# Convolutions and a wavelet layer on one core: a third buffer for stored results, kept sums in more tiles and asked for sooner, 12 ScalarE products in the first mixing

## The chip, the cores and the metric

The kernel runs on one core of one Trainium2 chip. The metric is the device time of one execution in microseconds (us); lower is better. TensorE (PE) multiplies matrices into PSUM, VectorE (DVE) and ScalarE (ACT) do elementwise work, GpSimd (POOL) does a little of it, and SyncE (SP) issues most of the DMAs; ACT issues the rest.

## The reference

The input is `x` of shape (4, 64, 256, 256): 4 batches of 64 channels of 256x256 images. Four layers follow each other. Layers 0, 1 and 3 are long convolutions whose kernel is separable (an outer product of two filters that a small network makes); layer 2 is a thresholding in the Haar wavelet domain that mixes channels. Cut to what matters:

```python
# layers 0, 1 and 3, for each channel
k = hx[:, None] * hy[None, :]                 # separable 256x256 kernel
y = irfft2(rfft2(x, 512x512) * rfft2(k, 512x512) / 512)[:256, :256]
x = y + x * bias[:, None, None]

# layer 2
f1 = haar2d(x)
acc = 0
for i in range(2):
    f4 = einsum('bchw,oc->bohw', f1 * v[i], conv_w[i])
    acc += sign(f4) * relu(abs(f4) - tau[i])
x = haar2d(acc, inverse=True) + x
```

## The kernel before, in words

Each convolution is written as two products with Toeplitz matrices, one for each axis. `contract` (L250) does one product of a 256x256 channel as four matmuls into one PSUM bank; `toeplitz` (L241) loads the filter's matrix, 256 KB, with a DMA on SP. `first` (L256) is the product of the first axis (`pa`) and ScalarE's copy of it to SBUF (`a`, L267). `second` (L271) is the product of the second axis (`py`) and the residual sum on VectorE (`y`, L284), which writes a tile of the tag that it is given, with `BUFS[tag]` buffers.

The work has three kinds of stages.

- `convolutions(b, ...)` does layers 0 and 1 of batch b, channel by channel, and the forward Haar transform. `pairs` (L327) splits the result into sums and differences of neighbours; `store` (L332) keeps both in DRAM (`keep`) for the inverse. `levels` goes on with the row transform, `split` and `rest` divide the values into two parts for TensorE, `down` transforms the columns, and `away` (L382) copies the coefficients from PSUM into a tile of tag "co" (L385) and stores them from SP (L386).
- `mixing(b, ...)` does the mixing of channels and the threshold in 64 groups of positions. It loads `f` (tag "f", 3 buffers, L423), multiplies by the channel matrix into PSUM (`px`, L441), and scales the 16 products of a group: `scaled` (L458) on VectorE takes the first 16 - n_act of them in one instruction (L460), `scaled_too` (L462) on ScalarE takes the other n_act with one activation of 128x64 each (L465). The results are in `f4` (tag "f4", 2 buffers). `size`, `sign`, `shrink`, `signed` and `add` finish the threshold. n_act comes from `N_ACT`, one number for each batch.
- `inverse(b, ...)` transforms back and does layer 3. For each channel, `sooner` asks for the filter, `early` (L513) loads the kept sums `r` (L515), `fetch` copies the coefficients on ScalarE (`zc`, L525), `rows` transforms them on TensorE (`pw`, L532 and L533), and `join` (L552) on VectorE adds the kept sums and makes the image `u` (L554, L557, L558). For the first 16 channels `halves` (L536, tag "f4") and `cols` come in between. Then layer 3 follows: product, copy, product, sum (L284, into tag "co" again), and the store of the output from ACT's queue (L602). In batches 0 to 2 every third channel is put off: its `u` goes to DRAM from ACT's queue (L562), and layer 3 for it is done beside the last mixing (`convolution`, L605).

The stages of different batches overlap. While batch b is mixed, the convolutions of batch b+1 are worked off beside it, and their last coefficients are formed during the inverse of batch b.

The order of the work is written out as events. Each step is entered with `at(time, run, unit)`; the time is the tick of its channel or group plus an offset from the table `PLACE` (L26). The events are sorted by time and run, and that gives each instruction its rank. A planner in the framework then simulates the engines with its own costs and lets an instruction pass others of its queue where these are not ready or their buffer is not free yet. So a `PLACE` is a rank and not a promise, and a change of buffers can move other instructions too. On the chip each engine and each DMA queue works in the planned order and waits by semaphores. Tiles of one tag take turns in its buffers; a new tile waits until the last use of the old one has ended.

For `early`, `PLACE` is counted from the channel's tick c after the inverse begins. `join` stands at c + 1.433, and one tick later for the first 16 channels. The same tag "f" with its 3 buffers serves the mixing's loads and the kept sums of the inverse.

Of the kernel before, what the change touches and what calls it, by code (L numbers as in the profile page):

```python
# [9 lines left out]
F32 = mybir.dt.float32  # L10
# [7 lines left out]
P = 128  # L18
ROW = S + P

GT = 4
BUFS = {"res": 1, "y": 5, "co": 2}

N_ACT = (14, 12, 12, 6)

PLACE = {  # L26
    "load": 0.714,
# [22 lines left out]
    "shrink": 1.777,  # L50
    "signed": 2.802,
    "add": 3.331,
    "sooner": -0.8,
    "early": -0.4,
    "fetch": 0.414,
    "rows": 1.071,
    "halves": 1.522,
# [41 lines left out]
def conv_seq_kernel(ctx, tc, x, fz, fw, bias, decay, haar, haar_row, factors, vt, taut, wmix, out):  # L99
# [14 lines left out]
    nc = tc.nc  # L114
# [8 lines left out]
    mx = ctx.enter_context(tc.tile_pool(name="mx", bufs=2))  # L123
# [117 lines left out]
    def toeplitz(layer, c, name):  # L241

        t = tp.tile([P, 2, S], F32, name=name, tag="toep")
        nc.sync.dma_start(t, ap(pads[layer], c * 2 * ROW, [[1, P], [ROW, 2], [1, S]]))
        return t
# [25 lines left out]
    def second(b, st, key, layer, res, new, tag, ahead=None):  # L271
# [9 lines left out]
        def residual(c):  # L281
            s = st[c]
            y = io.tile([P, 2, S], F32, name=f"{new}_{b}_{c}", tag=tag, bufs=BUFS[tag])
            nc.vector.scalar_tensor_tensor(y, s[res], bsb[:, layer, c : c + 1], s["p" + new], ALU.mult, ALU.add)  # L284
# [9 lines left out]
    def level(n, chunk, begin=0, count=None):  # L294

        count = n if count is None else count
        v = z.rearrange("p n s x c -> p n s (x c)")[:, chunk].rearrange("p (j e s) x -> p j e s x", e=2, s=P // 2 // n)
        halve(v[:, begin : begin + count, 0, 0, :], v[:, begin : begin + count, 1, 0, :])

    def butterfly():  # L300

        v = z.rearrange("p n s (h k) c -> p n s h k c", k=2)
        for h in range(2):
            halve(v[:, :, 0, h, 0, :], v[:, :, 0, h, 1, :])
# [6 lines left out]
    def at(time, run, unit):  # L311
        events.append((time, len(events), run, unit))

    def convolutions(b, ticks, in_parts=(), border=None):
# [67 lines left out]
        def away(c):  # L382
            t = io.tile([P, 2, S], F32, name=f"co_{b}_{c}", tag="co", bufs=BUFS["co"])
            ps = parts.pop(("ps", c)).rearrange("p e (k w) -> p e k w", k=2)
            nc.scalar.copy(t.rearrange("p k (e w) -> p e k w", e=2), ps)  # L385
            nc.sync.dma_start(coef[b][:, c].rearrange("k p w -> p k w"), t)  # L386
# [122 lines left out]
    def inverse(b, start, put_off):  # L509

        st = {}

        def early(c):  # L513
            r = mx.tile([P, 2, 2, P], F32, name=f"r_{b}_{c}", tag="f", bufs=3)
            nc.sync.dma_start(r, keep[b][c])  # L515
            st[c]["r"] = r

        def sooner(c):
            st[c] = {}
            if c not in put_off:  # L520
                st[c][2] = toeplitz(2, c, f"t2_{b}_{c}")

        def fetch(c):
            a = mx.tile([P, 2, 2, P], F32, name=f"zc_{b}_{c}", tag="mag")
            nc.scalar.copy(a.rearrange("p h k i -> p (h k) i"), z[:, c // 16, :, :, c % 16].rearrange("p i x -> p x i"))  # L525
            st[c]["z"] = a

        def rows(c):
            a = st[c]["z"]
            ps = psx.tile([P, 2, 2, 2, P], F32, name=f"pw_{b}_{c}", tag="mix")[:, 0]  # L530
            for m in range(2):
                nc.tensor.matmul(ps[:, 0, m, :], a[:, 0, m, :], hsinv, start=True, stop=True)  # L532
                nc.tensor.transpose(ps[:, 1, m, :], a[:, 1, m, :], ident)  # L533
            st[c]["pw"] = ps

        def halves(c):  # L536
            w = st[c]["w"] = mx.tile([P, 2, 2, 2, P], F32R, name=f"w_{b}_{c}", tag="f4")
            ps = st[c]["pw"]
            nc.scalar.copy(w[:, 0], ps)  # L539
            nc.vector.tensor_tensor(w[:, 1], ps, w[:, 0].bitcast(F32), ALU.subtract)  # L540

        def cols(c):
            ps = psm.tile([P, 2, 2, P], F32, name=f"pu_{b}_{c}", tag="mm")
            flat = "p e m w -> p (e m w)"
            for i in range(2):
                nc.tensor.matmul(
                    ps.rearrange(flat), hb, st[c]["w"][:, i].rearrange(flat), start=(i == 0), stop=(i == 1)
                )
            st[c]["pw"] = ps

        def join(c):
            ps = st[c]["pw"]  # L552
            t = io.tile([P, 2, 2, P], F32, name=f"t_{b}_{c}", tag="res", bufs=BUFS["res"])
            nc.vector.scalar_tensor_tensor(t, st[c]["r"], 0.5, ps, ALU.mult, ALU.add)  # L554
            u = io.tile([P, 2, S], F32, name=f"u_{b}_{c}", tag="y", bufs=BUFS["y"])
            v = u.rearrange("p m (w e) -> p m w e", e=2)
            nc.vector.tensor_add(v[:, :, :, 0], t[:, 0], t[:, 1])  # L557
            nc.vector.tensor_sub(v[:, :, :, 1], t[:, 0], t[:, 1])  # L558
            st[c]["u"] = u

        def aside(c):
            nc.scalar.dma_start(late[b, c], st.pop(c)["u"])  # L562

        along = start - groups - 3

        def when(tick, n, chunk, *span):
            at(tick + PLACE["level"], lambda _: level(n, chunk, *span), 0)

        at(along + 11 + PLACE["level"], lambda _: butterfly(), 0)
        for chunk in range(1, 4):  # L570
            turn = start + 16 * (chunk - 1)
            for n in (1, 2, 4, 8):
                when(along + 12 + 3 * chunk if b + 1 < B else turn, n, chunk)
            when(turn + 1, 16, chunk)
            for i in range(2):
                when(turn + 2 + 2 * i, 32, chunk, 16 * i, 16)
            for i in range(4):
                when(turn + 6 + 2 * i, 64, chunk, 16 * i, 16)

        for c in range(C):  # L580
            for name, stage in zip(("sooner", "early", "fetch", "rows"), (sooner, early, fetch, rows)):
                at(start + c + PLACE[name], stage, c)
            turn = start + c
            if c < 16:
                at(start + c + PLACE["halves"], halves, c)
                at(start + c + PLACE["cols"], cols, c)
                turn += 1
            at(turn + PLACE["join"], join, c)
            if c in put_off:
                at(turn + PLACE["aside"], aside, c)  # L590
            else:
                shift = (0.0, 0.0)
                if put_off:
                    shift = ((-0.27, -0.342), (0.23, 0.158))[c % 3]
                for name, stage in zip(("a3", "a3 copy", "y3", "y3 sum", "out"), last(b, st)):
                    at(turn + PLACE[name] + shift[name[0] != "a"], stage, c)

    def last(b, st):
        return [
            *first(b, st, "u", 2, "a3"),  # L600
            *second(b, st, "a3", 2, "u", "y3", "co"),
            lambda c: nc.scalar.dma_start(out[b, c].rearrange("(k p) w -> p k w", p=P), st.pop(c)["y3"]),  # L602
        ]
# [42 lines left out]
    for b in range(B):  # L646
        mixing(b, start, N_ACT[b])
        end = start + groups + 3
# [124 lines left out]
```

## Time and profile before

| what | value |
|---|---|
| time, median of 3 runs | 2897.4 us (2896.96 to 2901.36) |
| profiled execution, own time | 2897.57 us |
| its span, first to last instruction | 2895.8 us |
| instructions in it | 52461 |
| PE busy | 2825.5 us |
| DVE busy | 2501.4 us |
| ACT busy | 2082.3 us |
| POOL busy | 335.3 us |
| HBM traffic over the span | 223 GB/s |
| granted TensorE clock | 0.999 of full speed |

The span is that of one profiled execution, and the time around it is the launch and the end. Busy time of an engine is the time in which at least one of its instructions runs; "idle before" is the time that the engine stood before an instruction, and a releaser is what ended that wait by the semaphores. SPq and ACTq are the DMA issues of these two queues. The stages follow each other in the trace: mixing 0 from 446 to 865 us, inverse 0 to 1067, mixing 1 to 1518, inverse 1 to 1726, mixing 2 to 2177, inverse 2 to 2378, mixing 3 to 2666, and inverse 3 to the end.

### The profile page before, as it was taken

The page shows a single profiled execution, that of the slowest core. Times are in us where ns is not written, and L with a number is a line of the kernel's source. Part 1 is how long each engine was busy: PE and PEld are TensorE (multiplying, and loading weights), DVE is VectorE, ACT ScalarE, POOL GpSimd, SP SyncE. Part 2 cuts the span into 40 slices and gives each one's busy share as a digit, 9 for nine tenths or more (in the row PEclk, how much of TensorE's full clock was granted, in tenths as well). Part 3 has the DMA queues.
Part 4 walks back from the last instruction along what each step waited for, and adds up shares of the span by engine and source line. Part 5 has one row for each costly group of instructions (what it writes and reads, how often), then busy time and mean ns, then how long its engine had stood idle before and what let it go on. Part 6 is the DMA issues. An engine that isn't in the chain of part 4 may idle for free. (4 is left out here: it accounts for less than half of the span.)

```text
span 2895.8 us, 52461 instructions
## 1 busy us (share of the span) xinstructions
PE 2825.5 (98%) x16566; PEld 2548.3 (88%) x16566; DVE 2501.4 (86%) x4263; ACT 2082.3 (72%) x4950; POOL 335.3 (12%) x644
## 2 busy tenths in 40 slices
PE   8999999999999999999999899999999999999999
PEld 6999998888888898998888898998888898888998
DVE  4656558999999779999998679999999779999985
ACT  2333338999995558989985558989995558888554
POOL 0111111121121001221211001121121000000000
PEclk9999999999999999999999999999999999999999
DMA  5877777666677886777777886777767888777776
GB/s 163 261 231 231 231 232 223 207 202 207 194 209 225 271 260 199 215 211 212 208 214 234 258 265 196 214 212 211 212 207 235 269 276 239 230 237 208 217 239 207
DMA packets 599368, 649.78 MB, mean 224 GB/s; under 512 B 48465, under 2 KB 517044, under 8 KB 598964
## 3 DMA queue, kind: packets, MB, share of 16 engines
q1 hardware_dynamic: 519860, 562.09, 65.9%
q10 hardware_dynamic: 79232, 84.34, 8.3%
q8 instruction: 134, 2.20, 0.3%
q14 instruction: 142, 1.16, 0.1%
HBM read 426.77 MB, written 219.48 MB: 223 GB/s over the span
## 5 line engine op out<-in xcount | busy, mean ns | idle before, releaser
L253 PE MATMUL py<-t,a 128*128 128x256 f32 x3072 | 924.1, 383 | 18.6 <-ACT a L267 18.0
L267 ACT COPY a<-pa 128x512 f32<-128x512 f32 x768 | 492.0, 641 | 510.8 <-PE pa L254 450.4
L465 ACT ACTIVATE f<-px,vt 128x64 f32<-128x64 f32 x2816 | 623.1, 410 | 95.0 <-DVE f L460 94.7
L254 PEld LDWEIGHTS py<-t,a 128*128 128x128 f32 x3072 | 584.0, 190 | 79.6
L254 PE MATMUL py<-t,a 128*128 128x128 f32 x3072 | 590.5, 274 | 0.0
L253 PEld LDWEIGHTS py<-t,a 128*128 128x128 f32 x3072 | 495.9, 191 | 62.9 <-ACT a L267 31.7
L441 PE MATMUL px<-wb,f 128*128 128x256 f32 x2048 | 490.4, 381 | 11.9 <-ACT f L465 11.7
L441 PEld LDWEIGHTS px<-wb,f 128*128 128x128 f32 x2048 | 367.8, 190 | 57.2 <-ACT f L465 18.4
L343 POOL TENSOR_TENSOR sd<-less 128x128 f32<-128x128 f32 (+4 forms) x320 | 187.4, 586 | 1874.9 <-DVE less L342 1535.2
L525 ACT COPY zc<-z 128x512 f32<-128x512 f32 x256 | 281.4, 1103 | 106.9 <-PE pw L533 93.4
L476 DVE TENSOR_TENSOR mag<-mag,vt 128x1024 f32<-128x1024 f32 x256 | 317.0, 1238 | 10.2 <-ACT mag L469 9.4
L469 ACT ACTIVATE mag<-f 128x1024 f32<-128x1024 f32 x256 | 304.7, 1190 | 22.1 <-DVE z L486 21.6
L480 DVE SCALAR_TENSOR_TENSOR mag<-mag,f 128x1024 f32<-128x1024 f32 x256 | 317.1, 1240 | 0.1
L253 PE MATMUL pa<-t,y 128*128 128x256 f32 x1024 | 308.3, 383 | 5.8 <-DVE y L284 5.0
L253 PE MATMUL pa<-t,x 128*128 128x256 f32 x1024 | 305.8, 380 | 0.0
L366 DVE TENSOR_TENSOR sp<-sd,sp 128x512 fp32r<-128x512 f32 x256 | 179.9, 703 | 132.3 <-ACT sp L361 130.6
L472 ACT ACTIVATE f<-f 128x1024 f32<-128x1024 f32 x256 | 291.8, 1140 | 3.1
L253 PE MATMUL pa<-t,u 128*128 128x256 f32 x772 | 231.9, 382 | 4.4 <-ACT w L539 2.9
L284 DVE SCALAR_TENSOR_TENSOR y<-x,bsb,py 128x512 f32<-128x512 f32 x256 | 190.5, 744 | 41.2 <-PE py L254 40.2
L254 PEld LDWEIGHTS pa<-t,y 128*128 128x128 f32 x1024 | 194.5, 190 | 26.3
L254 PEld LDWEIGHTS pa<-t,x 128*128 128x128 f32 x1024 | 194.6, 190 | 26.3
L284 DVE SCALAR_TENSOR_TENSOR y<-y,bsb,py 128x512 f32<-128x512 f32 x256 | 190.4, 744 | 27.8 <-PE py L254 27.8
(72 smaller groups left out, 4426.3 us busy)
## 6 DMA issues: line engine op xcount, KB each, us to landing
t<-pad SPq DMA_DIRECT2D x768, 256.0 KB, 4.0
x<-in_x SPq DMA_DIRECT2D x256, 256.0 KB, 3.8
coef<-co SPq DMA_DIRECT2D x256, 256.0 KB, 3.2
f<-coef SPq DMA_DIRECT2D x256, 256.0 KB, 3.1
r<-keep SPq DMA_DIRECT2D x256, 256.0 KB, 3.9
out_y<-y ACTq DMA_DIRECT2D x256, 256.0 KB, 4.0
keep<-sums SPq DMA_DIRECT2D x256, 128.0 KB, 2.8
keep<-sd SPq DMA_DIRECT2D x256, 128.0 KB, 2.8
```

The source lines that it names most:

```text
L253: nc.tensor.matmul(ps[:, m, :], src[:, 0, m * P : (m + 1) * P], t[:, ::-1], start=True, stop=False)
L254: nc.tensor.matmul(ps[:, m, P:], src[:, 1, m * P : (m + 1) * P], t[:, : P - 1 : -1], start=False, stop=True)
L267: nc.scalar.copy(a, s["p" + new])
L284: nc.vector.scalar_tensor_tensor(y, s[res], bsb[:, layer, c : c + 1], s["p" + new], ALU.mult, ALU.add)
L343: engine.tensor_tensor(t[:, :, :, half:length], v[..., 0], v[..., 1], ALU.subtract)
L441: nc.tensor.matmul(ps[:, q, h, :], f[:, q, h * P : (h + 1) * P], wb.rearrange("p r n -> p (r n)"), start=True, stop=True,)
L465: nc.scalar.mul(f4[:, j], px[:, j], scale(g, 0)[:, j : j + 1])
L469: nc.scalar.activation(mag, st[g]["f4"], AF.Abs)
L472: nc.scalar.activation(st[g]["f4"], st[g]["f4"], AF.Sign)
L476: nc.vector.tensor_sub(mag, mag, over(g, 1, 16))
L480: nc.vector.scalar_tensor_tensor(mag, mag, 0.0, st[g]["f4"], ALU.max, ALU.mult)
L525: nc.scalar.copy(a.rearrange("p h k i -> p (h k) i"), z[:, c // 16, :, :, c % 16].rearrange("p i x -> p x i"))
```

## The change

Five edits are made together.

- The tag "co", which serves the forward coefficients and the results of layer 3, has three buffers and not two.
- In the mixing of batch 0, ScalarE scales 12 of a group's 16 products and VectorE 4; before it was 14 and 2. The other batches stay at 12, 12 and 6.
- From channel 20 of an inverse on, two of five tiles for the kept sums are taken from the tag "f4" (2 buffers), which is idle there once the first 16 channels have passed `halves`; the other three still are taken from "f" (3 buffers).
- `sooner` (the filter of layer 3) moves from 0.8 to 1.2 ticks ahead of its channel, and `early` (the kept sums) from 0.4 to 1.0.
- The size of the scratch for dynamic DMAs, which lies in SBUF, is halved from 2048 to 1024.

```diff
 GT = 4
-BUFS = {"res": 1, "y": 5, "co": 2}
+BUFS = {"res": 1, "y": 5, "co": 3}
 
-N_ACT = (14, 12, 12, 6)
+N_ACT = (12, 12, 12, 6)
...
     "add": 3.331,
-    "sooner": -0.8,
-    "early": -0.4,
+    "sooner": -1.2,
+    "early": -1.0,
     "fetch": 0.414,
...
         def early(c):
-            r = mx.tile([P, 2, 2, P], F32, name=f"r_{b}_{c}", tag="f", bufs=3)
+            tag, bufs = ("f", 3) if c < 20 or c % 5 < 3 else ("f4", 2)
+            r = mx.tile([P, 2, 2, P], F32, name=f"r_{b}_{c}", tag=tag, bufs=bufs)
             nc.sync.dma_start(r, keep[b][c])
             st[c]["r"] = r
...
-    nc = _bacc.Bacc("TRN2", target_bir_lowering=False, num_devices=1, dynamic_dma_scratch_size=2048)
+    nc = _bacc.Bacc("TRN2", target_bir_lowering=False, num_devices=1, dynamic_dma_scratch_size=1024)
```

## The prediction

> **What bounds the kernel now.** I read the shares of each engine first, then a table of busy time by stage, then the waits, and last the timeline around the longest of them. The page's first part says which engine to watch:
>
> ```profile
> PE 2825.5 (98%) x16566; PEld 2548.3 (88%) x16566; DVE 2501.4 (86%) x4263; ACT 2082.3 (72%) x4950; POOL 335.3 (12%) x644
> ```
>
> TensorE idles 2895.8 - 2825.5 = 70.3 us of the span. (The ends of matmuls are modelled, so gaps of a few tenths of a us are hidden in it; the true reserve is somewhat larger.) About 14 us of it lie in the first 68 us, before the change acts. Where the rest lies is in the table of stretches: length, then busy us of PE, PEld, DVE, ACT and POOL. The rows are mixing 0, inverse 0, mixing 1, inverse 1, mixing 2, inverse 2, mixing 3, inverse 3.
>
> ```profile
> 446.00:865.00 419.00, 410.08 (x2258) 361.48 (x2257) 409.14 (x690) 407.98 (x1229) 80.37 (x130) 1.00 0.69 205
> 865.00:1067.00 202.00, 192.28 (x1251) 175.85 (x1250) 162.43 (x299) 116.42 (x153) 7.73 (x20) 1.00 0.83 257
> 1068.00:1518.00 450.00, 447.62 (x2516) 403.15 (x2516) 437.76 (x729) 398.33 (x1118) 90.08 (x140) 1.00 0.70 208
> 1518.00:1726.00 208.00, 198.42 (x1276) 181.33 (x1275) 160.63 (x300) 118.57 (x158) 7.62 (x20) 0.99 0.83 257
> 1727.00:2177.00 450.00, 447.54 (x2515) 403.01 (x2514) 437.88 (x729) 398.56 (x1119) 88.03 (x140) 1.00 0.70 208
> 2177.00:2378.00 201.00, 194.25 (x1258) 177.69 (x1257) 159.63 (x298) 117.48 (x156) 7.62 (x20) 1.00 0.85 263
> 2378.00:2666.00 288.00, 279.00 (x1516) 248.48 (x1515) 285.18 (x408) 245.67 (x574) 0.00 (x0) 1.00 0.78 233
> 2666.00:2891.00 225.00, 222.29 (x1456) 205.55 (x1456) 190.19 (x325) 116.12 (x145) 0.00 (x0) 1.00 0.72 218
> ```
>
> Three regimes show. Mixing 1 and 2 are TensorE's: it idles 2.4 us in 450. Mixing 0, the one stage with 14 products on ScalarE, has three engines within 11 us of full: PE idles 8.9, DVE 9.9, ACT 11.0. Inverses 0, 1 and 2 leave PE idle for 9.7 + 9.6 + 6.75 = 26.1 us although neither DVE nor ACT is full, so something there waits. The waits of the whole run name it (total, times, longest):
>
> ```profile
> DVE y L284 <- DMA out_y<-y: 23.3, 14, 5.4
> ...
> DVE y L284 <- DMA coef<-co: 4.4, 3, 1.6
> ...
> DVE t L554 <- DMA r<-keep: 1.1, 1, 1.1
> ```
>
> The y3 sum of L284 waits until an earlier tile of tag "co" has been stored: 17 times, 27.7 us, nearly all in those inverses. The third line is the kept sums: they come too late once. The timeline of inverse 1 shows what the store costs others (brackets: idle time before, and what ended it):
>
> ```profile
> 1648.57 0.38 ACTq L602 DMA_DIRECT2D out_y<-y  x1
> ...
> 1656.59 0.75 DVE L284 SCALAR_TENSOR_TENSOR y<-u,bsb,py 128x512 f32<-128x512 f32 x1 [5.37 <-DMA out_y<-y]
> 1657.26 0.68 DVE L554 SCALAR_TENSOR_TENSOR t<-r,pw 128x512 f32<-128x512 f32 x1
> 1657.37 0.38 ACTq L602 DMA_DIRECT2D out_y<-y  x1
> 1657.79 0.59 ACT L267 COPY a<-pa 128x512 f32<-128x512 f32 x1 [4.95 <-DVE y L284]
> ...
> 1658.43 1.22 PE L253 MATMUL py<-t,a 128*128 128x256 f32 x2 [4.78 <-ACT a L267]
> ```
>
> One late store holds DVE 5.37 us; ACT's next issue of a store (L602) waits for that sum, the copy of the next a3 (L267) stands behind it on ACT, and PE waits 4.78 us for the copy.
>
> **What the skill says.** The Trainium skill, Perfetto Trace Analysis, section "Identifying Performance Opportunities", says that a gap which repeats on the engine that should be saturated can mean too few buffers for the next tile. The trace agrees: one tag with two buffers, some five such waits in each of inverses 0 to 2. The same page, "Optimizing Scalar/DVE Operations", suggests moving work from a saturated DVE to ScalarE; the change goes the other way, in a stage where DVE is at 97.6%. "VectorE: DVE Perf Modes", section "The TRN2 errata", prices a PSUM-sourced instruction at 120 + elements cycles at 0.96 GHz, so an estimate of 133 ns for 128 elements more; the trace says 139, which I use. "SBUF — State Buffer", section "SBUF size: 192, 224, or 256?", describes the DMA scratch as the software descriptor ring's. The page's list of queues here has hardware and instruction queues only, so I cost the halved scratch at nothing: nothing uses it.
>
> **Part 1, a third "co" buffer.** Added: memory; no instruction. A store lands 2.1, 4.0 and 7.3 us (least, median, most) after its issue. In an inverse a channel takes 202/64 = 3.2 us and two of three make a y3, so one comes each 4.7 us on average, less where neighbours follow and where the forward transform's coefficients ("away") take the same tag. Two buffers give a store about one such interval, three about two, over 9 us, more than the longest landing. So nearly all of the 27.7 us of DVE waiting should go. On PE only what follows counts. PE is stopped by the two routes from a held DVE: L253 py waiting for ACT's copy, 1.5 + 6.5 + 2.5 = 10.5 us in inverses 0, 1, 2; and L532 pw waiting for the join L554, which frees its PSUM bank, 3.1 + 0.5 + 1.8 = 5.4. Together 15.9 us. Some of these have other causes (a copy behind a store that waited for nothing but was issued late, a join that waited for its own matmul), so I take two thirds: **-10.6 us**. Ends: -4.8, the one stall shown above, to -16, all of both. Next late will be the join's wait for L533 pw (19.3, 19.8 and 16.8 us in the three inverses), which is PE's own pace.
>
> **Part 2, 12 products for 14 in mixing 0.** In its 64 groups ScalarE loses 2 activations each: 128, at 205.8/896 = 0.230 us of busy time, 29.4 us. L460 on DVE grows from 128x128 to 128x256: 284 to 423 ns in the groups by shape, so 64 x 0.139 = +8.9 us. ACT falls to 379 of 419 and is no bound; PE's waits for f L465 at px (6.9 us at the matmul, 12.2 at its weights, which overlap) should mostly go. But DVE rises to 418.0 in a stage of 419.0. What counts is how much of DVE's 9.9 us of idle time vanishes. Of it, 4.4 us waited for ACT's sp and 1.2 for ACT's mag, which a freer ACT returns. Mixing 3 shows DVE as sole bound: 2.8 us idle in 288, 1%. At that share the stage takes 409.1 + 8.9 + 4.2 = 422.2, **+3.2 us**. Upper end +8.9, if no idle time is recovered. Lower end below nothing: the inverse's levels (L291, L292) put 36.8 us of DVE work in 128x1024 pieces into this stage, and inverse 0 has 39.6 us of idle DVE; if enough of that moves later, PE bounds the stage, 410.1 plus mixing 1's idle share of 0.5%, 412: -7. I don't take that, since DVE is also full just after the stage (34.73 of 35 us up to 900).
>
> **Part 3, kept sums in the idle "f4" tiles, asked for sooner.** No transfer is added: 256 loads before and after. From channel 20 the loads rotate over five buffers, not three. Today the SP queue stands 311.5 us in total before L515 until a join frees a buffer, but only 1.1 us of that reaches a join, so I take **-1.1 us**. Asked for 0.6 places sooner, a load for a channel below 20 still waits for the join three channels back, and SP stands there longer. Queued behind it: the filters of L244, the inputs of L324, the stores of L333, L334 and L386. Nothing in the list of waits shows PE waiting for a filter, so this queue has slack; the filters asked for 0.4 sooner already wait for their buffer (371.6 us before L244 for py), and they gain nothing. Bounds: -4, if the planner, which places the joins by its own times for these loads, packs them better, to +4, if 20 loads in each of four inverses pass on 0.05 us.
>
> **Sum.** -10.6 + 3.2 - 1.1 = -8.5 us. The profiled execution took 2897.57 (span 2895.8 and 1.8 around it), 0.2 above the runs' median of 2897.4; from the latter it gives about **2889**.
>
> **Rivals.** *Slower: DVE-bound mixing.* The extra 139 ns in each group of mixing 0 lie bare: DVE's waits for ACT turn into waits for PE and stay 9.9 us, the batch-1 convolutions trail, and the lag runs into the DVE-full start of inverse 0: +8.9. With a store gain G this is a loss of over 0.2% (5.8 us) once G is below 3.1; at G = 1 it gives 2905. For it: the 99% of mixing 3. Against it: the 4.78 us stall alone exceeds 3.1. *Cancelled:* with the store out of the way, the sum L284 or the join waits for its product at the same place (21 us of L284's waits in these inverses already end with py), so -4 + 3 - 1: 2896. *Better packing:* the inverses lose half of their 26.1 us of PE idle time and the levels leave mixing 0: -13 - 7, 2877. *Not done:* if store waits of L284 remain, a third buffer was not what they wanted.
>
> **The numbers.** Forecast 0.55, better packing 0.15, cancelled 0.12, slower 0.18. About 0.08 of the forecast's share lies within 0.2% of the time before, which is about what a measurement of this kernel tells from no change: faster 0.62, same 0.20, slower 0.18. The forecast's own range, from the ends of part 1 with the middles of the rest, is 2883 to 2895; with both other cases' values inside, 2873 to 2904.
>
> **What would show it.** Right: L284's waits for out_y and coef under 5 us; PE idle in inverses 0 to 2 near 15 us; mixing 0 near 422 us with DVE over 98% busy and ACT near 90%; L460 at 423 ns in all of mixing 0; the SP queue's wait before L515 below 311.5. Wrong: mixing 0 at 428 or more; inverses as long as now; or PE waiting for t<-pad, which would mean that the loads asked for sooner block the queue.

## The result, and the profile after

The changed kernel takes 2877.64 us (median of 6 runs, 2874.14 to 2882.3) against 2898.33 us for the kernel before (6 runs, 2895.69 to 2901.36). The ratio is 0.993, with a 95% interval of 0.9918 to 0.9943: 20.7 us less by the medians. The forecast was -8.5 us.

The profiled execution of the changed kernel is the longest of its six: 2882.3 us, span 2880.5. Some 4 us of it were lost before mixing 0 began, in the first convolutions, where the two programs do the same work: from 100 to 200 us PE was busy for 97.5 of the 100 us, against 99.3 before, and for 3.4 of them it had half its clock (0.51 from 128.7 to 132.2). So stages are compared here, not ends. First the shares of the engines:

```profile
PE 2825.3 (98%) x16566; PEld 2553.6 (89%) x16566; DVE 2504.8 (87%) x4263; ACT 2057.4 (71%) x4822; POOL 333.1 (12%) x644
```

ACT has 128 activations fewer and 25 us less of busy time. PE's idle time is 2880.5 - 2825.3 = 55.2 us, 15.1 less than before. The table by stages (length, then busy us of PE, PEld, DVE, ACT, POOL) shows where. The rows are mixing 0, inverse 0, mixing 1, inverse 1, mixing 2, inverse 2, mixing 3, inverse 3, as before:

```profile
451.00:863.00 412.00, 406.30 (x2248) 362.49 (x2247) 404.19 (x681) 383.81 (x1100) 80.50 (x130) 1.00 0.70 208
863.00:1069.00 206.00, 197.66 (x1258) 179.67 (x1258) 171.45 (x307) 117.27 (x154) 10.02 (x20) 0.98 0.83 254
1070.00:1519.00 449.00, 446.76 (x2511) 402.49 (x2511) 437.05 (x726) 397.09 (x1118) 88.08 (x140) 1.00 0.71 208
1519.00:1717.00 198.00, 195.74 (x1275) 179.87 (x1274) 160.39 (x300) 119.11 (x158) 7.61 (x20) 1.00 0.86 271
1718.00:2168.00 450.00, 447.82 (x2517) 403.49 (x2516) 438.02 (x730) 397.31 (x1118) 88.04 (x140) 1.00 0.71 208
2168.00:2363.00 195.00, 192.80 (x1259) 177.34 (x1258) 159.32 (x299) 118.44 (x157) 7.61 (x20) 1.00 0.87 273
2363.00:2652.00 289.00, 279.74 (x1519) 249.02 (x1517) 286.19 (x411) 245.35 (x575) 0.00 (x0) 1.00 0.80 231
2652.00:2876.00 224.00, 221.73 (x1454) 205.64 (x1455) 189.62 (x322) 115.84 (x145) 0.00 (x0) 1.00 0.73 219
```

Inverse 1 lost 10 us and inverse 2 lost 6, and PE's idle time in inverses 0 to 2 is 8.3 + 2.3 + 2.2 = 12.8 us, where it was 26.1; mixings 1 to 3 and inverse 3 are the same within about 1 us. Mixing 0 lost 7 us by these rounded stretches, and inverse 0 gained 4. DVE's busy time in inverse 0 rose by 9.0 us, from 162.43 to 171.45, and in mixing 0 it fell by 5.0: work has gone over from mixing 0.

In the list of waits no row is left in which L284 waits for a stored tile of tag "co". A DMA row that grew is that of the kept sums (the line numbers after `early` are one higher in this kernel):

```profile
DVE t L555 <- DMA r<-keep: 8.0, 8, 1.0
```

### The profile page after: what moved, and what is told of

Read it like the earlier page. It is cut to its first block, busy times and chain, and to the rows that moved or that the text cites. A ratio compares the mean times of both kernels' runs of the same rounds, so it can differ in the third digit from the quotient of the medians.

```text
span 2880.5 us, 52311 instructions
## 1 busy us (share of the span) xinstructions
PE 2825.3 (98%) x16566; PEld 2553.6 (89%) x16566; DVE 2504.8 (87%) x4263; ACT 2057.4 (71%) x4822; POOL 333.1 (12%) x644
## 4 chain that ended last, share of the span: by engine, by line
PE 47%; DVE 12%; ACT 3%; DMA 3%; issue 2%; POOL 0%; SPq 0%; DVEq 0%; ACTq 0%
PE pa L253 12%; PE py L253 11%; PE px L441 6%; PE pa L254 6%; PE py L254 6%; PE pw L533 4%; DVE mag L480 2%; DVE mag L476 2%; DVE y L284 2%; ACT f L465 2%; PE pw L534 2%; PE pz L373 2%; DVE f L460 1%; DMA t<-pad 1%; DVE z L486 1%
## 5 line engine op out<-in xcount | busy, mean ns | idle before, releaser
L267 ACT COPY a<-pa 128x512 f32<-128x512 f32 x768 | 478.6, 623 | 501.2 <-PE pa L254 462.9
L465 ACT ACTIVATE f<-px,vt 128x64 f32<-128x64 f32 x2688 | 584.7, 367 | 106.1 <-DVE f L460 105.8
L469 ACT ACTIVATE mag<-f 128x1024 f32<-128x1024 f32 x256 | 295.4, 1154 | 22.9 <-DVE z L486 22.3
L366 DVE TENSOR_TENSOR sp<-sd,sp 128x512 fp32r<-128x512 f32 x256 | 178.7, 698 | 127.5 <-ACT sp L361 126.4
L472 ACT ACTIVATE f<-f 128x1024 f32<-128x1024 f32 x256 | 285.8, 1117 | 3.3
L284 DVE SCALAR_TENSOR_TENSOR y<-x,bsb,py 128x512 f32<-128x512 f32 x256 | 189.5, 740 | 44.6 <-PE py L254 43.6
L284 DVE SCALAR_TENSOR_TENSOR y<-y,bsb,py 128x512 f32<-128x512 f32 x256 | 189.3, 739 | 29.5 <-PE py L254 29.1
```

Source lines behind the costliest of these rows:

```text
L267: nc.scalar.copy(a, s["p" + new])
L465: nc.scalar.mul(f4[:, j], px[:, j], scale(g, 0)[:, j : j + 1])
L469: nc.scalar.activation(mag, st[g]["f4"], AF.Abs)
L472: nc.scalar.activation(st[g]["f4"], st[g]["f4"], AF.Sign)
```

## The experiments

The theory after the result was that the third buffer had won the 20 us alone, that the number of products had only moved work, and that the kept sums did nothing. The rivals were shares for the other two edits. Four kernels take the change apart.

**e1_co3: the third buffer alone, with the smaller scratch that makes room for it**

```diff
-BUFS = {"res": 1, "y": 5, "co": 2}
+BUFS = {"res": 1, "y": 5, "co": 3}
-dynamic_dma_scratch_size=2048
+dynamic_dma_scratch_size=1024
```

> The kernel before with the third co buffer alone (and the smaller scratch, which makes room for it). Store theory (the waits of L284 for a stored co tile were the main loss): these waits, 27.7 us, vanish, inverses 1 and 2 shorten by about 10 and 6 us as in the changed kernel, inverse 0 by about 6, mixing 0 stays at 418 us: 20 us less in all, ratio about 0.993. Rival (the kept sums asked for sooner did half of it): the store waits vanish, but the joins then wait for r<-keep, and only 8 to 12 us are won, ratio 0.996 to 0.997.

Measured: 2876.78 us against 2896.27, ratio 0.9934 (0.9922 to 0.9947). That is the whole gain. The order of the work hardly changed: compared by line, operation and tile name (without the tile's number), the trace has SP's order as it was, and 7 of DVE's 4263 rows and 19 of PE's 16566 stand elsewhere. So this run shows the waits and little besides. No run tests the scratch by itself; the profile after, like the one before, lists hardware and instruction queues only. The run's inverses 0, 1 and 2:

```profile
866.00:1064.00 198.00, 193.38 (x1260) 177.57 (x1259) 164.15 (x302) 117.99 (x155) 7.72 (x20) 1.00 0.85 264
1514.00:1712.00 198.00, 195.80 (x1277) 180.12 (x1276) 160.50 (x300) 119.00 (x158) 7.61 (x20) 1.00 0.87 270
2162.00:2358.00 196.00, 192.78 (x1254) 177.08 (x1253) 159.63 (x299) 118.00 (x156) 7.61 (x20) 1.00 0.86 269
```

PE's idle time in them is 4.6 + 2.2 + 3.2 = 10.0 us, where it was 26.1, and the three stretches sum to 592 us, where it was 611. The store waits are gone, and the joins don't wait for r<-keep for more than 0.4 us.

**e2_act12: 12 products alone**

```diff
-N_ACT = (14, 12, 12, 6)
+N_ACT = (12, 12, 12, 6)
```

> The kernel before with 12 for 14 products in mixing 0 alone. Prediction's price: mixing 0 grows by 3 us, ratio about 1.001. Rival A (three nearly full engines lose more to each other than one): mixing 0 shrinks by 6 us as in the changed kernel and inverse 0 stays: ratio 0.998. Rival B (work of VectorE only moves from mixing 0 into inverse 0): mixing 0 shrinks by 6 us, inverse 0 grows by as much or more, ratio 1.000 to 1.001.

Measured: 2895.46 us, ratio 0.9999 (0.999 to 1.0007). The interval leaves out Rival A's 0.998 and the price's 1.001. Mixing 0 and inverse 0:

```profile
448.00:860.00 412.00, 406.27 (x2248) 362.36 (x2248) 404.24 (x681) 383.82 (x1100) 80.52 (x130) 1.00 0.70 208
860.00:1067.00 207.00, 195.26 (x1255) 177.71 (x1254) 171.15 (x307) 117.29 (x154) 10.02 (x20) 0.99 0.81 251
```

They took 419 and 202 us before. Mixing 0 is 7 us shorter and inverse 0 is 5 longer, with 8.7 us more of DVE's work in it: Rival B, though inverse 0 grew by a little less than mixing 0 lost.

**e3_kept: the kept sums and the two places alone**

```diff
-    "sooner": -0.8,
-    "early": -0.4,
+    "sooner": -1.2,
+    "early": -1.0,
-tag="f", bufs=3
+tag, bufs = ("f", 3) if c < 20 or c % 5 < 3 else ("f4", 2)
```

> The kernel before with the kept sums in f4 tiles too and both PLACE edits alone, co at two buffers. Store theory: the store waits of L284 stay above 20 us and the time stays within 3 us, ratio 0.999 to 1.001. Rival (kept sums matter by themselves): 8 to 12 us less, ratio 0.996 to 0.997. Second rival (the queue of SP is blocked by loads asked for sooner): 5 us more.

Measured: 2895.58 us, ratio 1.0 (0.9991 to 1.0008). Its waits:

```profile
DVE y L284 <- DMA out_y<-y: 19.1, 16, 2.3
DVE t L555 <- DMA r<-keep: 11.3, 11, 1.5
```

L284 waits for stores of results nearly as before, 23.3 us there and 19.1 here (with those of coefficients 27.7 and 23.7). The joins wait longer for the kept sums than the 1.1 us of before, although these are asked for sooner. Neither shows in the time.

**e4_act14: the changed kernel with 14 products**

```diff
-N_ACT = (12, 12, 12, 6)
+N_ACT = (14, 12, 12, 6)
```

> The changed kernel with mixing 0 back at 14 products on ScalarE. If 12 products cost 3 us as predicted, this one is 3 us faster than the changed kernel, ratio to the kernel before about 0.992. If 12 products won the 6 us that mixing 0 lost, it is 6 us slower than the changed kernel, ratio 0.995. If work only moved between mixing 0 and inverse 0, it is equal to it, 0.993, with mixing 0 at 418 us and inverse 0 near 197.

Measured: 2875.38 us, ratio 0.9928 (0.9915 to 0.9942). Within the interval it equals the changed kernel; 0.995 is left out, but 0.992 is not. Mixing 0 took 417 us and inverse 0 took 197. What has moved is in the view of L291 (one instruction of each pair of level pieces): the first line is the changed kernel's mixing 0, the second its inverse 0, the third and fourth the same with 14 products.

```profile
L291 DVE TENSOR_TENSOR z<-z x25: 211/683/1220, 474.4 to 854.0; 128x1024 f32<-128x1024 f32 x11, 128x64 f32<-128x64 f32 x5, 128x128 f32<-128x128 f32 x3, 128x256 f32<-128x256 f32 x3
L291 DVE TENSOR_TENSOR z<-z x10: 1206/1216/1308, 869.6 to 939.1; 128x1024 f32<-128x1024 f32 x10
```
```profile
L291 DVE TENSOR_TENSOR z<-z x29: 216/1211/1418, 463.1 to 844.7; 128x1024 f32<-128x1024 f32 x15, 128x64 f32<-128x64 f32 x5, 128x128 f32<-128x128 f32 x3, 128x256 f32<-128x256 f32 x3
...
L291 DVE TENSOR_TENSOR z<-z x6: 1209/1212/1420, 871.6 to 898.1; 128x1024 f32<-128x1024 f32 x6
```

Four pairs of 128x1024, at twice 1.21 us 9.7 us of DVE work, left mixing 0 for inverse 0. My reading is that the planner uses the levels to fill gaps on DVE: with the larger L460 there are fewer gaps, and pieces stay over.

**s2_away_own: two buffers for the results, one for the coefficients**

```diff
 def away(c):
-    t = io.tile(..., tag="co", bufs=BUFS["co"])
+    t = io.tile(..., tag="cw", bufs=1)
-dynamic_dma_scratch_size=2048
+dynamic_dma_scratch_size=1024
```

> The kernel before with a tag of its own with one buffer for the coefficients of away, so that the results of layer 3 have two buffers for themselves: as many bytes as with the third co buffer. Sharing theory (the waits come where both users take turns; after 1000, 1656 and 2312 us, when the last coefficients have been formed, there were none): nearly all of the gain of the third buffer, 17 to 21 us, ratio 0.9928 to 0.9942. Rival (two buffers are too few for the results alone): store waits remain above 10 us and less than 12 us are won, ratio above 0.996. Third possibility: the single buffer holds ScalarE's copies L385 during mixing, and mixing 1 and 2 grow by some us each.

Measured: 2884.05 us, ratio 0.9961 (0.9948 to 0.9973), less of a gain than the sharing theory gave. Its inverses 0 to 2:

```profile
869.00:1065.00 196.00, 191.56 (x1251) 176.11 (x1250) 162.53 (x298) 116.67 (x153) 7.73 (x20) 1.00 0.85 265
1516.00:1713.00 197.00, 194.70 (x1270) 178.99 (x1269) 160.10 (x299) 118.33 (x157) 7.60 (x20) 1.00 0.87 269
2164.00:2361.00 197.00, 193.56 (x1259) 177.67 (x1259) 159.94 (x300) 118.51 (x157) 6.55 (x20) 1.00 0.87 269
```

They are as short as with three shared buffers, in the same order of the work on PE, DVE and SP. So two buffers are enough for the results alone, and the trouble was the sharing. The kernel before says the same: in its inverse 3 no coefficients are formed, 64 results come in 225 us, closer than in the other inverses, and two buffers cost L284 a single short wait (window 2666 to 2896):

```profile
DVE y L284 <- DMA out_y<-y: 0.8, 1, 0.8
```

But the time stands 7 us above the third shared buffer's. The waits of the whole run name a price:

```profile
ACT co L385 <- DMA coef<-co: 13.8, 10, 3.9
...
DVE y L284 <- DMA out_y<-y: 3.4, 4, 1.1
```

A single buffer holds L385, for 10.6 of the 13.8 us in the convolutions ahead of mixing 0, which began at 451.6 us, against 448.4 in e1_co3. But in the two profiles of the changed kernel, which has no such waits, it began at 450.7 and 449.2. The third possibility named mixing 1 and 2, and these did not grow. So where the 7 us arise is not shown.

**s1_sp_store and s5_pool_store: the output's store on another queue, "co" at two buffers.** These were to tell how much of the loss went over ACT's queue.

```diff
-lambda c: nc.scalar.dma_start(out[b, c]...)
+lambda c: nc.sync.dma_start(out[b, c]...)      # s1; nc.gpsimd in s5
```

> The kernel before, co at two buffers, with the store of the output issued from SP's queue and not from ACT's. The late store still holds the sum L284 on VectorE, but ScalarE's copies no longer stand behind an issue that waits for that sum. If the route over ACT's queue carries two thirds of the loss (10.5 of 15.9 us in the prediction), 10 to 14 us are won, ratio 0.995 to 0.9965, with store waits of L284 still near 20 us. Rival: VectorE's standstill itself, through the joins, carries it; then less than 4 us are won, ratio above 0.9985. A second rival: SP's queue, which loads everything, is now held by those sums, and it gets slower by 5 us or more.

> The kernel before, co at two buffers, with the store of the output issued from GpSimd's queue, which holds neither ScalarE's copies nor SP's loads. If the loss goes over ACT's queue (10.5 of 15.9 us in the prediction), 8 to 14 us are won although L284 still waits 20 us or more for stores: ratio 0.995 to 0.997. If VectorE's standstill carries it through the joins, the time stays within 4 us: ratio above 0.9985. If [...] the stores land later, L284 waits longer than 28 us and it is slower.

Measured: 2902.99 us, ratio 1.0023 (1.0014 to 1.0032), and 2918.29 us, ratio 1.0071 (1.0058 to 1.0084). Both are slower, and both leave the question open. In s1's inverse 1 the matmuls of py waited 0.3 us for ACT's copies, where it was 6.5; that route was cut. Yet PE's busy time in inverses 0 to 2 rose from 585 to 596 us with the same matmuls, which I read as more short waits inside it, and 240 of PE's 16566 rows stand elsewhere. In s5 the stores took 4.3 us to land, and L284 waited 27.9 us for stores of both kinds, the same as before. In both runs PE stood once for 13.0 us before pw at the end of mixing 3. The 6 us that s1 lost are what its second rival gave, but s5, whose stores are not on SP's queue, has the same order on PE and the same standstill, so SP's queue isn't shown to be the cause. The experiment changed the plan more than the wait that it was meant to cut.

**s3_levels: the levels of batch 0 ranked earlier, on the changed kernel**

```diff
-turn = start + 16 * (chunk - 1)
+turn = start + 16 * (chunk - 1) - ((12, 28, 44)[chunk - 1] if b == 0 else 0)
```

> The changed kernel with the ranks of batch 0's levels (L291, L292) moved ahead by 12, 28 and 44 ticks for chunks 1, 2 and 3, so that 7 more of their pairs (2.44 us each) run before the last add of mixing 0. If the cost of 12 products is VectorE work that only changes its place, mixing 0 grows by about 10 to 15 us to 422 to 427, inverse 0 shrinks to about 192, and the total stays within 3 us of the changed kernel, ratio 0.992 to 0.994. If the full start of inverse 0 was a bad place for them, 4 us or more are won against the changed kernel, ratio 0.9915 or less. If mixing 0 is the bad place, it is slower than the changed kernel by 4 us or more, ratio above 0.9945.

**s4_act10: 10 products**

```diff
-N_ACT = (12, 12, 12, 6)
+N_ACT = (10, 12, 12, 6)
```

> The changed kernel with 10 products on ScalarE in mixing 0, 9 us more on VectorE. In the planned order four more pairs of level pieces leave mixing 0. Displacement theory: mixing 0 gains no more than 2 us, since TensorE bounds it now, and inverse 0 grows by 8 us or more, so it is 6 to 9 us slower than the changed kernel, ratio 0.995 to 0.9965. Rival (fewer ScalarE products go on helping): mixing 0 loses another 5 us and the total stays or falls, ratio 0.993 or less.

Measured: s3_levels 2886.43 us, ratio 0.9969 (0.9957 to 0.9981); s4_act10 2877.65 us, ratio 0.9939 (0.9926 to 0.9951). Mixing 0 and inverse 0 of s3_levels, then of s4_act10:

```profile
449.00:878.00 429.00, 412.89 (x2272) 367.16 (x2270) 421.65 (x695) 386.88 (x1104) 80.40 (x130) 0.99 0.68 202
878.00:1071.00 193.00, 189.50 (x1226) 173.95 (x1227) 154.69 (x292) 114.61 (x150) 6.63 (x20) 0.99 0.84 265
```
```profile
447.00:854.00 407.00, 406.12 (x2257) 363.59 (x2256) 403.67 (x673) 361.27 (x973) 88.29 (x130) 1.00 0.71 210
854.00:1062.00 208.00, 196.84 (x1243) 178.69 (x1243) 177.89 (x314) 116.14 (x152) 9.58 (x20) 0.98 0.81 251
```

With 10 products, mixing 0 shrinks by 5 us more (PE idles 0.9 us of 407), and inverse 0 takes 2 us more. I had expected 6 to 9 us more in total, and it came out even, as the rival had it. So what is added to DVE's work in mixing 0 is not simply paid in inverse 0: there DVE is busy for 6.4 us more and the stage is 2 us longer. Forcing the levels back into mixing 0 is the bad move of the two: inverse 0 falls to 193 us, but mixing 0 grows by 17 us. At its end PE waits 6.4 us at once for L284 behind the levels, and soon after 4.1 us for `sp` (L366).

**r_after, r_act14, e9_act13: 12, 14 and 13 products, everything else as changed**

> The changed kernel once more, for a comparison on the same chip with 14 and 13 products: 0.993 again, and a mean stage pair of mixing 0 and inverse 0 near 616 us.

> The changed kernel with 14 products again. If the number of products only moves VectorE's work between mixing 0 and inverse 0, it is within 0.1% of the changed kernel. If 12 products cost the 3.2 us of the prediction, it is 3 us faster, and then it is the version that beats both kernels.

> The changed kernel with 13 products: 4.5 us of VectorE work less than with 12, two pairs of level pieces back in mixing 0. The theory that the work only moves gives the same time within 0.1%, with mixing 0 between 412 and 417 us and inverse 0 between 197 and 206.

Measured: 2878.86, 2879.6 and 2874.45 us; ratios 0.9936 (0.9924 to 0.9949), 0.9936 (0.9924 to 0.9949) and 0.9922 (0.9908 to 0.9935). The stage pairs in the profiles are 617, 613 and 612 us long. With 14, 13, 12 and 10 products, mixing 0 holds 15, 13, 11 and 7 of the 128x1024 pieces of L291, so the levels give way step by step. From 10 to 14 products no difference stands clear of the intervals. 13 has the lowest median, but no version here beats the changed kernel beyond doubt.

## Why the prediction was right, and where its steps were off

- **The total.** The measured 2877.6 us lies outside the forecast's own range (2883 to 2895) and inside the wider one (2873 to 2904), which takes in the rivals. The direction and the mechanism of the gain were right. The size was not: the forecast was less than half of it.
- **The waits of L284 for stores.** They were said to fall from 27.7 us to under 5; none is left. The mechanism, one tag with too few buffers, is shown by e1_co3, whose order of work is nearly that of before. It agrees with what the prediction drew from the Trainium skill, Perfetto Trace Analysis, section "Identifying Performance Opportunities", on gaps that repeat: here PE's idle time in inverses 0 to 2 fell from 26.1 to 10.0 us with a third buffer. That the two users of the tag get in each other's way was named as an aggravation only; s2_away_own shows that it was the cause.
- **The size of part 1.** The forecast was -10.6 us and its far end -16; e1_co3 measures -19.5. The term that failed is the 15.9 us of PE waits, of which I took two thirds. In e1_co3's inverses 0 to 2 the same two waits are 1.5 us, so 14.4 of the 15.9 came back, and PE's idle time fell by 26.1 - 10.0 = 16.0 us in all. Another 3.0 us came out of PE's busy time in the inverses (585.0 to 582.0). By the estimate in the last section, 1.7 of them are the half clock that followed the stall of 4.8 us; the rest may be short waits that the modelled ends hide. I had said of the whole span that the reserve is larger than the idle time, and did not apply it to this sum. The split of the loss between ACT's queue and the joins stays open.
- **Part 2.** L460 rose to 415 ns for 128x256 (423 was used), ACT fell to 383.8 us (379), and PE's waits at px fell from 6.9 to 1.4 us, as said. The step that failed is the length of the stage: 412 us and not 422. The prediction named the cause as its lower end, that the levels move to inverse 0, and rejected it because DVE is full there. Both halves were true: the stage shrank to that 412, and inverse 0 grew by 9 us against 14 products (206 and 197). The net is nothing that the times show (e2_act12), where +3.2 was forecast. With the third buffer the two stages together took 618 and 617 us with 12 products and 614 and 613 with 14 in the profiles, but the ratios of all runs are equal (0.9930 and 0.9936 with 12, 0.9928 and 0.9936 with 14); a cost of a us or two there is not excluded. DVE was never the sole bound of the two stages together: at 12 products it is busy for 575.6 of 618 us.
- **Part 3.** -1.1 us was forecast, and e3_kept gives none. SP's wait before the load of the kept sums fell from 311.5 to 262.7 us, as said, though the third buffer alone brings it to 285.0; and the joins' waits for them rose from 1.1 to 8.0 us. These small waits fall on DVE in stages where it has slack.
- **The rivals.** The total, 2878, is that of "better packing" (2877), but not its mechanism: it had given 13 us to the inverses and 7 to mixing 0, and mixing 0's gain was paid back in inverse 0. That the sums meet is luck. "Slower" fell with e1_co3 and e2_act12: the price of 8.9 us did not lie bare, and the store gain was six times the 3.1 us from which that rival decided. "Cancelled" fell too: L284's waits for its product rose only from 116.3 to 123.1 us.

## What to carry to other kernels

When two producers share a tag, count the buffers against both of them together, and over the time from a store's issue to its landing; a wait for a stored tile on an engine with slack can still cost much of its length on the engine without (here 27.7 us of waits cost 19.5). Before you charge a stage for added work, look for work in it that only fills gaps: that work can leave, and the bill, if one comes, comes in the next stage. And when a gain is added up from idle time alone, remember that the busy time of a pipelined engine can shrink as well, here by 3.0 us.

## What was not expected of the hardware

A stall of PE can cost more than its length. In the changed kernel the view by stretches gives, for two stalls of about 2.0 us and the 3.4 us that begin 1.1 and 0.5 us after them (length, busy us of PE, PEld, DVE, ACT, POOL, then the granted clock):

```profile
883.30:885.40 2.10, 0.16 (x2) 0.00 (x0) 2.10 (x4) 2.10 (x3) 0.00 (x0) 1.00 0.38 125
886.50:889.90 3.40, 3.40 (x13) 2.96 (x12) 2.43 (x3) 1.04 (x1) 0.00 (x0) 0.51 0.07 26
941.90:944.10 2.20, 0.28 (x3) 0.04 (x2) 2.17 (x6) 1.07 (x1) 0.00 (x0) 1.00 0.95 334
944.60:948.00 3.40, 3.40 (x13) 2.96 (x13) 2.35 (x6) 0.59 (x1) 0.00 (x0) 0.50 1.03 359
```

By estimate, 3.4 us at half the clock cost another 1.7 us. The 4.8 us stall of the kernel before, which the prediction showed, had the same after it (0.51 from 1658.0 to 1661.4), and that stall is gone. The length of the stall alone does not decide. One of 1.6 us ending at 992.2 in the kernel before was followed by the full clock. One of 1.9 us, at the same place in mixing 0, was followed by the full clock in e4_act14 (ending at 762.1) and by half of it in e1_co3:

```profile
760.40:762.40 2.00, 0.10 (x1) 0.00 (x0) 2.00 (x3) 2.00 (x11) 0.00 (x0) 1.00 0.62 175
763.10:766.50 3.40, 3.40 (x12) 2.89 (x11) 2.27 (x6) 3.40 (x10) 0.00 (x0) 0.50 0.23 77
```

What else decides is not shown by these runs. The two stretches at half clock in inverse 0 came with 12 products in both profiles of the changed kernel and with neither 13 nor 14. The 3.4 us that they cost by this estimate would be part of what inverse 0 grew.
